# A graph layer whose last node tile is cut to the last two buckets, with x's product made in mid-run

## The chip, the cores and the metric

The kernel runs on one core of one Trainium2 chip. The metric is the device time of one launch in microseconds. The kernel before took 1346.37 us (median of 3 runs, 1346.32 to 1348.4).

## What is computed

6,250 nodes with 128 features, 206,250 edges with 128 features, float32 throughout. `src` is not sorted (the edges come sorted by `dst`), so the sum over edges is a scatter-add.

```python
def ref(x, edge_index, edge_features, global_feat, W_c, b_c, W1, b1, W2, b2, W3, b3):
    row = edge_index[0]                                   # src
    edge_aggr = jnp.zeros((n, HIDDEN)).at[row].add(edge_features)
    global_expand = jnp.repeat(global_feat, reps, axis=0)
    combined = jnp.concatenate([x, edge_aggr, global_expand], axis=-1) @ W_c + b_c
    h = jax.nn.softplus(combined @ W1 + b1)
    h = jax.nn.softplus(h @ W2 + b2)
    return h @ W3 + b3
x = _layernorm(x + ref(...), axis=-1)
```

## The kernel before

*Stages.* Nodes are split into 32 buckets of `BL` = 196. Stage one sorts the edges by bucket and puts them into DRAM (`rows_by`): edges are loaded in blocks (`load_rows`), a one-hot matrix per column of 122 edges is built on VectorE and ScalarE (`compare`, lines 973 to 982), TensorE multiplies by it (`gather`, 993), ScalarE copies the sorted columns out of PSUM (`settle`, 1005: four copies for a piece of up to three pairs of columns), and GpSimd scatters each pair of columns with one indirect DMA (`scatter_row`, 1022), 846 in all. Where each edge goes is worked out beside that in steps of VectorE and TensorE (`positions`). The 846 pairs are in eight groups of 28, 72, 124, 124, 124, 128, 124 and 122.

Stage two sums. Chunks of 128 sorted rows of one bucket are read back (`load`, on SyncE's queue), up to eight chunks a load. `match` (lines 811 to 826) compares each row's place in its bucket with the numbers 0 to 195 and so makes a 128 x 196 one-hot tile (`hot`), for units of up to four chunks; `product` (845) multiplies chunk by one-hot tile on TensorE into PSUM; `add` (866, 868) adds the result to `sums_t`, which is held features by nodes. A visit takes what is there of two neighbouring buckets. Stage two begins while stage one still runs; the last visits to each bucket come after the last scatter, in the order of buckets.

Stage three is the layer, in `node_layers` (1157). Since nothing nonlinear lies between `W_c` and `W1`, they are multiplied once (`combine`, into `fold`), and the biases likewise (`biases`). A tile is 512 nodes: 12 tiles of 512 and one of 106. A tile goes through `z_of(1)` (two products: `fold[:, 0]` with x turned, line 1168, `fold[:, 1]` with the sums, line 1169), `decay` and `log1p` on ScalarE (1179, 1180, 1185: exp and log of softplus), `softplus` on VectorE (1193, gives h), `z_of(2)` (1172), the same again, then `last_layer`: the third product (1208), x added (1212), mean and variance (1215, 1219). Tiles are normed in parts of three, three, three, two and two: `norm` works out 1/sqrt on VectorE in 12 tiny instructions (1228 to 1236) and then scales. All but the last part are scaled by GpSimd (1250) and stored from GpSimd's queue (1254); the last part is scaled by VectorE and ScalarE in turns (1250, 1247) and stored from SyncE's queue.

*Order.* TensorE, VectorE, ScalarE and SyncE run in the order in which the program emits. In stages one and two each step has a nominal time, worked out in the file, and the steps are emitted by it: a scatter every 1.3 us from 24 us on, `over(steps, t0, t1)` spreads a list evenly over a stretch. `PREP` = 0.85 keeps the last 15% of each group's stretch free of `positions`; with `NODES = (3, 4)` the steps of `node_rows`, `combine` and `biases`, go into the last 15% of group 3. `weights` loads the layer's weights and all of x turned (`x_t`) at a nominal 100 us. What is left of stage two after the last scatter (`rest`) is emitted tile by tile: `summed_to(k)` emits it until all buckets that tile k needs are summed.

One step of the layer loop emits: z2 of the tile before, `decay` and `log1p` of this tile and the one before, `summed_to` and z1 of the next tile, both `softplus`, and the last layer (and at a part's end the norm) of the tile two before. So norms of the first four parts stand between the sums of one tile and those of the next.

*SyncE's queue* carries all loads of edges and of chunks, the fill of `rows_by`, the weights and `x_t`; ScalarE's carries x for the residual (`x_sb`, read at the end of stage one as four runs of 512 bytes a partition).

The compare of one unit reads the numbers from PSUM:

```python
                    nc.vector.tensor_tensor(
                        hot[:, q - a:q - a + m],
                        chunks[j][:, lo:hi + 1:step, D:W].to_broadcast([P, m, BL]),
                        iota_ps.unsqueeze(1).to_broadcast([P, m, BL]), op=ALU.is_equal)
```

Of the kernel before, what the change touches and what calls it, by code (L numbers as in the profile page):

```python
# [7 lines left out]
F32 = mybir.dt.float32  # L8
# [10 lines left out]
P = 128  # L19

BL = 196
# [48 lines left out]
NODES = (3, 4)  # L70
TURNED = 2048
# [20 lines left out]
WEIGHTS = (("wc0", P), ("wc1", P), ("wc2", P), ("w1", P), ("w2", P), ("w3", P), ("b3", P), ("cols", 4))  # L92

# [39 lines left out]
def kernel(  # L133
# [11 lines left out]
    real_edges: int,  # L145
):
# [8 lines left out]
    N, D = x.shape  # L155
# [82 lines left out]
    x_t = const.tile([P, N], F32, name="x_t")  # L238
# [25 lines left out]

    def node_rows_of(pool, n0, n, bufs, load=sync_dma):
        t = pool.tile([P, 4, D], F32, name="x_sb", bufs=bufs)
        for lo, hi, r in blocks_of(n):
            m0 = n0 + lo * P
            load(t[:r, lo:hi, :],
                 x[m0:m0 + (hi - lo) * r, :].rearrange("(b p) d -> p b d", p=r))  # L270
        return t
# [11 lines left out]
    with ExitStack() as phase:  # L283
# [462 lines left out]
        def sum_steps():  # L746
# [64 lines left out]
            def match(n):  # L811
                j, a, e = units_of[n]
                hot = hots.tile([P, HALF, BL], F32, name="hot")
                hots_of[n] = hot
                q = a
                while q < e:
                    lo = hi = place_in(j, q)
                    step, m = 1, 1
                    while q + m < e and place_in(j, q + m) > hi and (m == 1 or place_in(j, q + m) == hi + step):
                        step, hi = place_in(j, q + m) - hi, place_in(j, q + m)  # L820
                        m += 1
# [4 lines that stand above are left out]
                    q += m  # L826
# [70 lines left out]
        def node_rows():  # L897
# [32 lines left out]
            return [combine, biases]  # L930
# [103 lines left out]
        with tc.manual_schedule(engines={ET.PE, ET.DVE, ET.Activation, ET.SP}):  # L1034
# [78 lines left out]
            when(100.0, weights)  # L1113
# [11 lines left out]
            for g in range(G):  # L1125
# [31 lines left out]
    def node_layers(sums, ready):  # L1157

        tiles = [(n0, min(4 * P, N - n0)) for n0 in range(0, N, 4 * P)]
        parts = [tiles[i:i + 3] for i in range(0, len(tiles) - 4, 3)]  # L1160
        parts += [tiles[len(parts) * 3:-2], tiles[-2:]]
# [3 lines left out]
        def z_of(layer, n0, w):  # L1165
            z = bank()
            if layer == 1:
                nc.tensor.matmul(z[:, :w], fold[:, 0, :], x_t[:, n0:n0 + w], start=True, stop=False)
                nc.tensor.matmul(z[:, :w], fold[:, 1, :], sums_t[:, n0:n0 + w],  # L1169
                                 start=False, stop=True)  # L1170
            else:
                nc.tensor.matmul(z[:, :w], w_sb["w2"], h1.pop(n0)[:, :w], start=True, stop=True)
            sub_z[layer, n0] = [z]

# [48 lines left out]
        def norm(now, last):  # L1223
# [13 lines left out]
            if last:  # L1237

                minus = work.tile([P, 16], F32, name="minus")[:, :nb]
                nc.vector.scalar_tensor_tensor(minus, mv[:, :nb, 0], -1.0, g,  # L1240
                                               op0=ALU.mult, op1=ALU.mult)
            for n0, w, y, at in now["done"]:
                for lo, hi, r in blocks_of(w):
                    for q in range(lo, hi):
                        k = at + q
                        if last and q % 2:
                            nc.scalar.activation(y[:r, q, :], y[:r, q, :], AF.Identity,
                                                 bias=minus[:r, k:k + 1], scale=g[:r, k:k + 1])
                            continue
                        (nc.vector if last else nc.gpsimd).tensor_scalar(  # L1250
                            y[:r, q, :], y[:r, q, :], mv[:r, k, 0:1], g[:r, k:k + 1],
                            op0=ALU.subtract, op1=ALU.mult)
                    m0 = n0 + lo * P
                    (sync_dma if last else nc.gpsimd.dma_start)(  # L1254
                        out[m0:m0 + (hi - lo) * r, :].rearrange("(b p) d -> p b d", p=r),
                        y[:r, lo:hi, :])


        with tc.manual_schedule(engines={ET.PE, ET.DVE, ET.Activation, ET.SP}):
# [14 lines left out]
            z_of(1, *tiles[0])  # L1274
            for step in range(len(tiles) + 2):
# [91 lines left out]
def laid_out(inputs):  # L1367
# [21 lines left out]
    return {"x": x, "x_turned": np.ascontiguousarray(x.T), "src": nodes, "src_runs": np.ascontiguousarray(  # L1389
# [23 lines left out]
```

## Time and profile before

| | |
|---|---|
| median of 3 runs | 1346.37 us |
| profiled execution | 1352.41 us |
| its span in the profile | 1350.7 us |
| busy: PE, PEld | 1199.8 us (89%), 1129.8 us (84%) |
| busy: DVE, ACT, POOL | 1020.2 us (76%), 1059.8 us (78%), 884.8 us (66%) |
| HBM read and written | 239.37 MB, 140.79 MB |

PE is TensorE's products and PEld its weight loads, DVE is VectorE, ACT ScalarE, POOL GpSimd, SP SyncE; a q behind a name is the queue of that engine, where DMAs are issued. A float32 product shows as two matmul records. A row of a timeline is: start in us from the span's start, length in us, engine, line, operation, output<-inputs, shapes, count; in brackets how long the engine was idle before it and which work ended that. A row may merge several instructions of one line. In a row of a group the first number after the bar is busy time in us, the second the mean length of one in ns. In a row of a stretch: from and to, its length, then busy us and count for each engine, the granted TensorE clock (1.00 is full), the DMA share and GB/s.

The span falls into two parts: until about 1108 us the scatters run on POOL; from there to the end the remaining sums and the layer run on PE, DVE and ACT.

### The profile page before, as it was taken

How to read it: one execution, taken by the hardware profiler on the slowest of the kernel's cores; microseconds unless marked ns; L12 is line 12 of the kernel's file. 1: busy time of each engine (PE TensorE's matmuls, PEld its weight loads, DVE VectorE, ACT ScalarE, POOL GpSimd, SP SyncE). 2: the span in 40 equal slices, each digit the busy share in tenths (PEclk: the TensorE clock that was granted, in tenths of full speed). 3: DMA queues.
4: the chain of work that ended last, by engine and by line, in shares of the span. 5: the costliest groups of instructions: out<-in, count | busy, mean ns of one | idle time of the engine just before them, and what ended most of it. 6: DMA issues, size and time to landing. Idle time of an engine off the chain costs nothing. (4 is left out here: it accounts for less than half of the span.)

```text
span 1350.7 us, 26938 instructions
## 1 busy us (share of the span) xinstructions
PE 1199.8 (89%) x8677; PEld 1129.8 (84%) x8677; DVE 1020.2 (76%) x2366; ACT 1059.8 (78%) x2469; POOL 884.8 (66%) x919
## 2 busy tenths in 40 slices
PE   5767788899988899998999999999999989998893
PEld 4666777889988889898998989989989988887782
DVE  7969757877788478896888877798656668777775
ACT  5999899999999879899899999989999930222222
POOL 2777777777777777777777777777777772003115
PEclk9889889999999889999999999999989999998996
DMA  9889999999989879998999989999999996545431
GB/s 242 259 265 368 344 351 341 340 336 339 311 293 307 279 257 304 294 321 286 304 317 293 339 288 292 308 297 323 332 337 312 330 297 207 171 149 152 126 118 51
DMA packets 196396, 377.48 MB, mean 279 GB/s; under 512 B 26038, under 2 KB 79870, under 8 KB 195866
## 3 DMA queue, kind: packets, MB, share of 16 engines
q1 hardware_dynamic: 148030, 255.64, 61.4%
q0 software_dynamic: 41488, 116.18, 24.6%
q10 hardware_dynamic: 6732, 3.87, 0.9%
q8 instruction: 73, 1.20, 0.4%
q14 instruction: 73, 0.60, 0.1%
HBM read 239.37 MB, written 140.79 MB: 281 GB/s over the span
## 5 line engine op out<-in xcount | busy, mean ns | idle before, releaser
L1022 POOL DMA_INDIRECT rows_by<-pairs,pair x846 | 826.0, 976 | 281.6 <-issue 201.3
L845 PE MATMUL part<-hot,chunks 128*128 128x196 f32 x3576 | 685.9, 338 | 20.3 <-DVE hot L822 13.4
L845 PEld LDWEIGHTS part<-hot,chunks 128*128 128x128 f32 x3576 | 600.2, 195 | 31.6 <-DVE hot L822 15.2
L1005 ACT COPY pairs<-sorted 64x387 f32<-64x387 f32 (+2 forms) x1144 | 543.5, 475 | 54.1 <-PE sorted L993 31.7
L993 PE MATMUL sorted<-rows,sort_hot 122*128 122x129 f32 x3384 | 504.2, 289 | 67.5 <-ACT pairs L1005 61.1
L993 PEld LDWEIGHTS sorted<-rows,sort_hot 122*128 122x128 f32 x3384 | 452.5, 199 | 89.7 <-ACT pairs L1005 86.1
L822 DVE TENSOR_TENSOR hot<-chunks,both_ps 128x392 f32<-128x392 f32 (+3 forms) x647 | 438.9, 710 | 30.5 <-PE part L845 19.4
L980 ACT ACTIVATE sort_hot<-plain,slot 122x128 f32<-122x128 f32 x846 | 278.3, 391 | 11.6 <-DVE slot L519 5.7
L868 DVE TENSOR_TENSOR sums_t<-sums_t,part 128x392 f32<-128x392 f32 (+1 forms) x163 | 89.5, 549 | 135.8 <-PE part L845 134.3
L982 ACT ACTIVATE sort_hot<-sort_hot,ones 122x384 f32<-122x384 f32 (+2 forms) x286 | 174.6, 610 | 9.3
L973 DVE TENSOR_TENSOR sort_hot<-slot,both_ps 122x384 f32<-122x384 f32 (+2 forms) x286 | 154.1, 541 | 13.5 <-PE sorted L993 7.5
L1179 ACT ACTIVATE away<-sorted,z_bias 128x512 f32<-128x512 f32 (+1 forms) x13 | 8.6, 660 | 184.2 <-PE sorted L1169 184.2
L1250 POOL TENSOR_SCALAR y<-y,mv,rs 128x128 f32<-128x128 f32 x44 | 34.3, 787 | 174.9 <-issue 102.4
L519 DVE TENSOR_REDUCE slot<-small 122x16 f32<-122x512 f32 (+2 forms) x109 | 72.9, 669 | 35.3 <-PE small L502 34.8
L623 DVE TENSOR_TENSOR past<-both_ps,starts 128x512 f16<-128x512 f32 (+2 forms) x110 | 71.9, 663 | 6.0 <-PE small L638 4.2
L441 DVE TENSOR_TENSOR pair_ib<-pair_block,both_ps 122x512 bf16<-122x512 bf16 (+2 forms) x109 | 71.7, 663 | 0.2
L502 PEld LDWEIGHTS <-starts_h 128*122 128x122 bf16 x423 | 43.0, 141 | 18.8 <-issue 9.9
L500 PE MATMUL small<-pair_ib,half 122*122 122x512 bf16 (+2 forms) x109 | 43.0, 394 | 7.2 <-DVE slot L519 7.2
L502 PE MATMUL small<-half,starts_h 128*122 128x128 bf16 x423 | 43.6, 226 | 0.0
L638 PEld LDWEIGHTS <-past 128*128 128x128 f16 x424 | 25.7, 99 | 18.9 <-DVE past L623 13.2
L638 PE MATMUL small<-jump,past 128*128 128x56 f16 (+3 forms) x424 | 29.2, 190 | 12.9 <-DVE past L623 9.6
L452 PE MATMUL small<-ones_h,pair_ib 122*128 122x48 bf16 x423 | 16.7, 186 | 12.7 <-DVE pair_ib L441 12.7
(128 smaller groups left out, 463.3 us busy)
## 6 DMA issues: line engine op xcount, KB each, us to landing
rows<-in_edge SPq DMA_DIRECT2D x105, 903.0 KB
chunks<-rows_by SPq DMA_DIRECT2D x158, 272.0 KB
chunks<-rows_by SPq DMA_DIRECT2D x60, 408.0 KB
chunks<-rows_by SPq DMA_DIRECT2D x69, 340.0 KB
chunks<-rows_by SPq DMA_DIRECT2D x131, 136.0 KB
rows_by<-pairs,pair POOLq DMA_INDIRECT x846
rows_by<-fill SPq DMA_DIRECT2D x21, 544.0 KB
rows<-in_edge SPq DMA_DIRECT2D x105, 80.6 KB
```

Of the source, the lines that this page charges most:

```text
L502: nc.tensor.matmul(pr[:, q * QUAD * NB:(q + 1) * QUAD * NB], own["starts_h"][:, q0 + q:q0 + q + 1].to_broadcast([KB, PN]), ident_h[:KB, :K ...
L519: nc.vector.tensor_reduce(to, of, axis=mybir.AxisListType.X, op=ALU.max)
L623: nc.vector.tensor_tensor(past[:, :, a:b], twice_ps[:KB].unsqueeze(1).unsqueeze(1).to_broadcast([KB, 2, b - a, P // 2]), own["starts"][:, ...
L822: nc.vector.tensor_tensor(hot[:, q - a:q - a + m], chunks[j][:, lo:hi + 1:step, D:W].to_broadcast([P, m, BL]), iota_ps.unsqueeze(1).to_bro ...
L845: nc.tensor.matmul(part[:, b - base_of[v], :], t[:, place_in(j, q), :D], hot[:, q - a], start=first, stop=last)
L868: nc.vector.tensor_add(here, here, of)
L973: nc.vector.tensor_tensor(hot[:PN, :m], slot[:PN, at:at + 2 * m - 1:2].unsqueeze(2).to_broadcast([PN, m, P]), slot_ps[:PN].unsqueeze(1).to ...
L980: nc.scalar.activation(hot[:PN, j], by_slot[:PN], AF.Abs, bias=slot[:PN, at:at + 1], scale=-1.0)
L982: nc.scalar.activation(hot[:PN, :m], hot[:PN, :m], AF.Relu, bias=ones[:PN, :1], scale=-1.0)
L993: nc.tensor.matmul(out[:, j, :], hot[:PN, j], rows_at[col // LOAD_COLS][:PN, col % LOAD_COLS, :], start=True, stop=True)
L1005: nc.scalar.copy(sets_at[i][64 * n:64 * n + 64, lo:lo + m, h, :W], out[64 * h:64 * h + 64, :m, :])
L1022: s = nc.gpsimd.indirect_dma_start(out=dst, out_offset=bass.IndirectOffsetOnAxis(ap=at, axis=0), in_=rows[:, j].rearrange("p a b -> p (a b ...
```

## The change

1. The node tiles: 11 of 512, one of 248 that ends where bucket 30 begins (node 5880), and a last one of 370 nodes, the last two buckets. Parts: four of three tiles, and the last tile alone.
2. x's product with `fold[:, 0]` leaves `z_of(1)`. It is made for 512 nodes at a time in mid-run (`times`), copied to SBUF as `x_f` (`times2`), and added to the product of the sums on VectorE (`with_x`) before ScalarE takes it; that addition is emitted behind the two `softplus` of the step before. x turned is loaded in 13 pieces (`fetch`), each two products ahead, into three buffers.
3. The steps of `node_rows` now go into the last 15% of groups 2 and 3: `combine`, two loads, `biases` and six products in group 2, seven products in group 3. The weights are loaded at a nominal 20 us.
4. Norms of the first four parts scale on ScalarE (an activation with scale and bias for each block of 128 nodes) and are stored from ScalarE's queue; GpSimd has no part in them. In the last part odd blocks are VectorE's and even ones ScalarE's.
5. Once all scatters are emitted, `match` makes one `tensor_scalar` for each chunk, with the numbers 0 to 195 in SBUF, where it made one `tensor_tensor` for up to four chunks.
6. x for the residual and the result lie in DRAM by blocks of 128 nodes, so that a tile's load or store is one run of up to 2 KB a partition. The host lays them out before and after.

```diff
-NODES = (3, 4)
-TURNED = 2048
+NODES, WEIGHTED = (2, 4), 20.0
+def node_tiles(n):
+    late = (-(-n // BL) - 2) * BL
+    assert 0 < n - late <= 4 * P
+    return [(a, min(4 * P, late - a)) for a in range(0, late, 4 * P)] + [(late, n - late)]
...
+    def in_blocks(of, n0, lo, hi, r):
+        at = next(k for k, (a, _) in enumerate(blocks) if a == n0 + lo * P) - lo
+        return of[:r, at + lo:at + hi, :]
...
+                if len(scattered) == TB:
+                    for q in range(a, e):
+                        at = place_in(j, q)
+                        nc.vector.tensor_scalar(hot[:, q - a], iota_f[:, :BL], chunks[j][:, at, D:W],
+                                                None, op0=ALU.is_equal)
+                    return
...
-            return [combine, biases]
+            of = {}
+            spans = [(a, min(N, a + 4 * P)) for a in range(0, N, 4 * P)]
+
+            def fetch(k):
+                a, b = spans[k]
+                of[k] = per.tile([P, 4 * P], F32, name="x_turned", bufs=3)[:, :b - a]
+                sync_dma(of[k], x_turned[:, a:b])
+
+            def times(k):
+                small = small_bank().rearrange("p b n -> p (b n)")[:, :spans[k][1] - spans[k][0]]
+                nc.tensor.matmul(small, fold[:, 0, :], of.pop(k), start=True, stop=True)
+                of["times", k] = small
+                if k + 2 < len(spans):
+                    fetch(k + 2)
+
+            def times2(k):
+                nc.vector.tensor_copy(x_f[:, slice(*spans[k])], of.pop(("times", k)))
+
+            steps = [combine, lambda: fetch(0), lambda: fetch(1), biases]
+            for k in range(len(spans)):
+                steps += [lambda k=k: times(k), lambda k=k: times2(k)]
+            return steps
...
-                for a in range(0, N, TURNED):
-                    b = min(N, a + TURNED)
-                    sync_dma(x_t[:, a:b], x_turned[:, a:b])
...
-            when(100.0, weights)
+            when(WEIGHTED, weights)
...
-                    upto = len(nodes)
+                    upto = len(nodes) if g + 1 == NODES[1] else 4 + (len(nodes) - 4) // 4 * 2
...
-        tiles = [(n0, min(4 * P, N - n0)) for n0 in range(0, N, 4 * P)]
-        parts = [tiles[i:i + 3] for i in range(0, len(tiles) - 4, 3)]
-        parts += [tiles[len(parts) * 3:-2], tiles[-2:]]
+        tiles = node_tiles(N)
+        parts = [tiles[i:i + 3] for i in range(0, len(tiles) - 1, 3)] + [tiles[-1:]]
...
-                nc.tensor.matmul(z[:, :w], fold[:, 0, :], x_t[:, n0:n0 + w], start=True, stop=False)
-                nc.tensor.matmul(z[:, :w], fold[:, 1, :], sums_t[:, n0:n0 + w],
-                                 start=False, stop=True)
+                nc.tensor.matmul(z[:, :w], fold[:, 1, :], sums_t[:, n0:n0 + w], start=True, stop=True)
...
+        def with_x(n0, w):
+            z = work.tile([P, 4 * P], F32, name="z_x", bufs=3)
+            nc.vector.tensor_add(z[:, :w], sub_z[1, n0][0][:, :w], x_f[:, n0:n0 + w])
+            sub_z[1, n0] = [z]
...
                         if last and q % 2:
+                            nc.vector.tensor_scalar(y[:r, q, :], y[:r, q, :], mv[:r, k, 0:1],
+                                                    g[:r, k:k + 1], op0=ALU.subtract, op1=ALU.mult)
+                        else:
                             nc.scalar.activation(y[:r, q, :], y[:r, q, :], AF.Identity,
                                                  bias=minus[:r, k:k + 1], scale=g[:r, k:k + 1])
-                            continue
-                        (nc.vector if last else nc.gpsimd).tensor_scalar(
-                            y[:r, q, :], y[:r, q, :], mv[:r, k, 0:1], g[:r, k:k + 1],
-                            op0=ALU.subtract, op1=ALU.mult)
-                    m0 = n0 + lo * P
-                    (sync_dma if last else nc.gpsimd.dma_start)(
-                        out[m0:m0 + (hi - lo) * r, :].rearrange("(b p) d -> p b d", p=r),
-                        y[:r, lo:hi, :])
+                    (sync_dma if last else nc.scalar.dma_start)(
+                        in_blocks(out, n0, lo, hi, r), y[:r, lo:hi, :])
...
                 for layer, tile_ in ((1, first), (2, second)):
                     if tile_:
                         softplus(layer, *tile_)
+                if step + 1 < len(tiles):
+                    with_x(*tiles[step + 1])
```

More of the change, by code (lines that the diff above doesn't have):

```diff
@@ L145 @@
     real_edges: int,
+    n_nodes: int,
 ):
     nc = tc.nc
-    N, D = x.shape
+    N, D = n_nodes, x.shape[2]
+    blocks = node_blocks(N)
     E = src.shape[0]
@@ L236 @@
     cols = of_weights["cols"]
-    x_t = const.tile([P, N], F32, name="x_t")
+    x_f = const.tile([P, N], F32, name="x_f")
     fold = const.tile([P, 2, D], F32, name="fold")
@@ L1236, in norm @@
                 nc.vector.scalar_tensor_tensor(g, t, 1.5, g, op0=ALU.add, op1=ALU.mult)
[L1237 to L1241, printed above, removed]
+            minus = work.tile([P, 16], F32, name="minus", bufs=2)[:, :nb]
+            nc.vector.scalar_tensor_tensor(minus, mv[:, :nb, 0], -1.0, g, op0=ALU.mult, op1=ALU.mult)
             for n0, w, y, at in now["done"]:
@@ L1274, in node_layers @@
             z_of(1, *tiles[0])
+            with_x(*tiles[0])
             for step in range(len(tiles) + 2):
```

21 lines of the change are left out of this document (14 added, 7 removed).

## The prediction

> **What bounds the kernel now.** First the groups and the waits, to see who sets the pace while edges are still being sorted. Columns of a group: busy us, mean ns | idle before, releaser.
>
> ```profile
> span 1350.7 us, 26938 instructions
> L1022 POOL DMA_INDIRECT rows_by<-pairs,pair x846 | 826.0, 976 | 281.6 <-issue 201.3
> POOL rows_by L1022 <- DVE much L585: 23.0, 2, 22.7
> ```
>
> The 846 scatters take (826.0 + 281.6 - 23.0) / 846 = 1.282 us each, and beyond the 23.0 us at the start POOL waits for almost nothing: its gaps are its own issue. So POOL sets the pace until the last scatter at 1107.9. Next the stretches (length, then busy us of PE, PEld, DVE, ACT, POOL; granted clock, DMA share, GB/s):
>
> ```profile
> 1000.00:1050.00 50.00, 49.58 (x347) 48.39 (x345) 33.34 (x57) 48.26 (x114) 38.10 (x40) 1.00 0.98 323
> 1140.00:1320.00 180.00, 168.19 (x883) 149.51 (x882) 133.85 (x286) 41.75 (x64) 23.44 (x30) 0.96 0.48 146
> ```
>
> After the scatters PE is busy 93% and DVE 74%: PE sets the tail. The timeline shows one step of it (start, length, engine, line, idle before):
>
> ```profile
> 1305.68 0.56 DVE L868 TENSOR_TENSOR sums_t<-sums_t,part 128x392 f32<-128x392 f32 x1 [1.07 <-PE part L845]
> 1306.47 1.02 PE L1168 MATMUL sorted<-x_t,fold 128*128 128x512 f32 x2
> 1307.33 1.02 PE L1169 MATMUL sorted<-sums_t,fold 128*128 128x512 f32 x2
> 1308.19 1.05 PE L1208 MATMUL small<-weights_sb,h 128*128 128x128 f32 x8
> 1309.08 1.02 PE L1172 MATMUL sorted<-h,weights_sb 128*128 128x512 f32 x2
> 1309.28 0.69 DVE L1212 TENSOR_TENSOR y<-small,x_sb 128x512 f32<-128x512 f32 x1 [1.72 <-PE small L1208]
> 1309.94 1.16 PE L845 MATMUL part<-hot,chunks 128*128 128x196 f32 x6
> 1311.07 1.41 DVE L822 TENSOR_TENSOR hot<-chunks,both_ps 128x588 f32<-128x588 f32 x2
> 1311.91 6.21 PE L845 MATMUL part<-hot,chunks 128*128 128x196 f32 x36 [0.81 <-PE part L845]
> ```
>
> A 512-wide product holds PE 0.86 us (1306.47 to 1307.33), a chunk 2 x 6.21 / 36 = 0.345 us. At a step's end DVE adds, forms both h, waits 1.72 us for the last-layer product, and only then makes the hot tiles that PE needs. Once the sums are done (the add at 1318.15) a latency chain runs to the end:
>
> ```profile
> 1318.15 0.56 DVE L868 TENSOR_TENSOR sums_t<-sums_t,part 128x392 f32<-128x392 f32 x1 [2.42 <-PE part L845]
> 1341.56 0.88 ACT L1247 ACTIVATE y<-y,minus,rs 128x128 f32<-128x128 f32 x2 [10.38 <-DVE minus L1240]
> 1342.46 0.88 SPq L259 DMA_DIRECT2D out<-y  x2
> 1344.79 0.81 POOL L1254 DMA_DIRECT2D out<-y  x1 [0.30 <-POOL y L1250]
> ```
>
> POOL is last, 2.3 us after SP; from its end (1345.6) to the end of the span are 5.1 us.
>
> **The change, part by part.** *x's product leaves the tail.* PE drops one 0.86 us product per tile; for the ten tiles 0 to 9 that is -8.6 us. DVE gains one addition per tile (`with_x`), by the row of L1212 0.69 us. It fits: the product taken away shortens DVE's 1.72 us wait to 0.86, and the addition needs only the first product, done before the second h. So DVE, too, reaches `y` 0.86 us earlier, and the whole step moves forward. What hides the addition is that wait; without it each step would give 0.69 back. Bounds: -8.6 with the cover whole, -1.7 with none; I take -8.6, since the wait stands in every step with a last layer.
>
> *The product's new place.* 13 products (11 us of PE), 13 copies out of PSUM (by L1212 some 0.69 us each) and 13 loads on SP's queue come into the last 15% of groups 2 and 3, six in the first window (about 291 to 315 us) and seven in the second; combine and biases move there from the second. POOL is the bound there, so the cost is nothing while sorted pairs are ahead of it. Counting ACT's copies (four for a piece of three pairs; 136 copies hold the first 100 pairs) against scatters started, from the windows of those two lines:
>
> ```profile
> 0.00:300.00 300.00, 142.05 (x298) 0.93 0.98 316
> 0.00:300.00 300.00, 209.61 (x215) 0.93 0.98 316
> 290.00:300.00 10.00, 9.12 (x60) 8.43 (x60) 5.03 (x10) 9.68 (x25) 7.56 (x9) 1.00 1.05 356
> 300.00:310.00 10.00, 8.48 (x61) 8.48 (x62) 6.07 (x13) 9.63 (x24) 7.56 (x9) 1.00 1.06 342
> 460.00:470.00 10.00, 8.71 (x59) 8.38 (x57) 1.93 (x8) 8.54 (x21) 7.56 (x9) 0.93 0.84 275
> 467.13 0.16 DVE L917 TENSOR_TENSOR z_bias<-small,weights_sb 128x1 f32<-128x1 f32 x1 [9.17 <-PE small L916]
> 469.03 0.29 DVE L928 TENSOR_TENSOR b_all<-small,weights_sb 128x128 f32<-128x128 f32 x1 [0.58 <-PE small L927]
> ```
>
> 100 + 3 x 162 / 4 = 221.5 pairs are copied at 300 us, 215 scatters started: six pairs, 7.7 us ahead. Six products (5.2 us) and the bias chain (some 2 us, from 467.1 to 469.0) less PE's 2.4 us of slack in 20 us put PE about 5 us behind. A wait on an SP load would come on top: PE stands at `times(k)` with the sorting behind it, which ACT's copies and then POOL need. Loads are asked for two steps, about 6 us, ahead. Bounds 0 to +7; I take 0, since the lead is larger than what is counted. The weights' load moves from 98.8 us to about 13 us, needed only at 291: nothing. In place of one load of x at 99 us the same bytes come in 13: nothing, POOL did not wait then or now.
>
> *One compare per chunk in the tail.* `match` replaces one instruction for up to four chunks, with the table in PSUM, by one `tensor_scalar` per chunk with the table in SBUF. Nearest is another one-pointer `tensor_scalar` on f32 in SBUF, among `tensor_tensor` of the same size:
>
> ```profile
> 15.81 0.24 DVE L609 TENSOR_SCALAR jump<-plain,far 128x56 f16<-128x56 f32 x1
> 15.97 0.21 DVE L605 TENSOR_TENSOR jump<-earlier,plain 128x56 f16<-128x56 f32 x1
> 567.76 0.34 DVE L609 TENSOR_SCALAR jump<-plain,far 128x256 f16<-128x256 f32 x1
> 568.02 0.42 DVE L605 TENSOR_TENSOR jump<-earlier,plain 128x256 f16<-128x256 f32 x1
> 568.36 0.35 DVE L609 TENSOR_SCALAR jump<-plain,far 128x256 f16<-128x256 f32 x1
> 1300.40 4.21 DVE L822 TENSOR_TENSOR hot<-chunks,both_ps 128x588 f32<-128x588 f32 x7
> ```
>
> From its start to the next one's: 0.16 us for 56 columns, 0.26 for 256, so 0.13 + 0.0005 a column; 196 columns take 0.23 us. `tensor_tensor` takes 0.34 for 256 (568.02 to 568.36), twice the slope. Today seven instructions make 18 chunks in 4.21 us, 0.234 each. A tie: 0. [...]
>
> *Norms and stores on ACT.* For each of the four whole parts ACT gets 10 or 12 scale-and-bias activations and the stores; POOL gets none. Two L1247 in 0.88 us, the second about 0.39 after the first: 12 x 0.39 + three stores at 0.44 issue (SP's two took 0.88) and a short drain, 0.55 each: 6.4 us. Norms 1 and 2 come ahead of the next steps' six activations in ACT's order; those need 4.1 us and are due after 42 chunks (14.5 us), so 10.5 us is covered. The third is not covered: it sits before the last activations.
>
> *The end, laid out anew.* The 12th tile (248 nodes) needs only buckets to 29, the 13th the last two. PE's order becomes: six chunks, product of the 12th, last layer of the 9th, z2 of the 11th, 15 chunks of the last two buckets, product of the 13th. Twelve of those 15 wait for hot tiles that DVE makes behind the third norm, and the last sums, the 13th's product and all of the end wait for them. A norm today:
>
> ```profile
> 1276.81 0.17 DVE L1235 SCALAR_TENSOR_TENSOR rs<-rs 128x12 f32<-128x12 f32 x1
> 1277.01 0.17 DVE L1236 SCALAR_TENSOR_TENSOR rs<-rs 128x12 f32<-128x12 f32 x1
> 1277.92 16.17 PE L845 MATMUL part<-hot,chunks 128*128 128x196 f32 x78 [3.33 <-DVE hot L822]
> 1318.63 0.75 DVE L1193 SCALAR_TENSOR_TENSOR h<-sorted,neg_z,away 128x512 f32<-128x512 f32 x1
> 1319.94 0.69 ACT L1179 ACTIVATE away<-sorted,z_bias 128x512 f32<-128x512 f32 x1 [7.45 <-PE sorted L1169]
> 1321.95 0.67 ACT L1179 ACTIVATE away<-sorted,b_c 128x512 f32<-128x512 f32 x1
> ```
>
> PE stands 3.33 us and then makes 78 matmuls in 16.17 us where 36 take 6.21: 2.7 us lost to the clock too. In today's clock, from the add at 1305.68 on: h of the 10th and 11th tiles, its z addition, `y` and statistics bring DVE to 1316.6, the norm (13 at 0.205) to 1319.3; first hot unit 1320.1; PE, idle 3.9 us and then slow, ends the 12 chunks about 1327.2 (1318.1 today). ACT norms from 1319.3 to 1325.9, then two activation triples (1.4 us for 248 columns, 2.05 for 512, as 1319.94 to 1321.95) to 1329.35, which is later than PE: h to 1330.05, z of the 13th 1330.6, its triple (1.7) 1332.3, the 12th's 1333.75, `y` of the 11th 1336.15, h of the 13th 1336.75, two blocks 1338.5, norm 1341.2, three blocks 1343.2, norm 1346.0; ACT meanwhile norms ten blocks with four stores (6 us) to 1347.2, two more blocks 1348.1, SP's stores to about 1348.7. That is 3.1 us after POOL's 1345.6. With the same 5.1 us behind it: +3.1. Bounds: +0.8 (today's end need not have waited for SP, whose last store left 2.3 us before POOL's, so 5.1 us behind it may be 2.8) to +6 (0.44 for each activation and 0.88 for each store, in both last norms).
>
> Sum: -8.6 + 0 + 0 + 3.1 = -5.5 us on the 1350.7 us span, 1345.2. The profiled execution took 1352.4 in all, 6.0 over the median of 1346.37; the runs should move by the same -5.5: 1340.9.
>
> **Rivals.** [...]
>
> ```profile
> [...]
> 24.12 0.28 DVE L569 TENSOR_SCALAR most_of<-much 128x1 f32<-128x1 f32 x3
> 48.97 0.15 DVE L569 TENSOR_SCALAR most_of<-much 128x1 f32<-128x1 f32 x1
> ```
>
> [...]
>
> B, no change: mid-run stall. If the loads of x land later than 6 us, each makes PE stand; 1.5 us at each of 13 uses up the lead by some 9 + 5 - 7.7 = 6.3 us in a window, and POOL never catches up: 1347. For: DMA share 1.05 there. Against: the lead.
>
> C, faster: a compare costs only 0.065 beside its columns, as a one-column L569 does (three in 0.28, one in 0.15), so 0.065 + 0.10 = 0.17. Hot units come 0.19 us sooner in ten steps: -1.9, 1339.0. [...]
>
> D, it does not do what it says: PE's freed time is given back to DVE's in-order waits; only the end's +3.1 stays: 1349.5.
>
> **Chances.** Forecast 0.52 (its own range 1336 to 1345), A 0.10, B 0.14, C 0.14, D 0.10. Range 1335 to 1351: it leaves out A and the edges of the forecast. A difference under 0.2% (2.7 us) can't be told from none. Faster 0.70 (forecast, C and some of B), same 0.12 (most of B), slower 0.18 (A, D).
>
> **What will show it.** The last scatter still ends at 1108 +-1 (else B). A tail step loses 0.86 us of PE with no new wait. [...] ACT's third norm ends after PE's last chunk, the last chunk ends near 1318.6, about where it ends now, and the last store leaves SP near 1340. I am wrong if the step before the third norm does not come some 8 us earlier, or if the stretch from the last chunk to the end does not shrink from 32.6 us to about 27.

## The result and the profile after

| | before | after |
|---|---|---|
| median of five runs, us | 1348.4 (1346.32 to 1348.99) | 1360.59 (1355.11 to 1362.0) |
| after / before, 95% interval | | 1.0077 (1.0056 to 1.0099) |
| span of the profiled execution, us | 1350.7 | 1360.0 |
| last scatter ends, us | 1108.9 | 1121.4 |
| from there to the end of the span, us | 241.8 | 238.6 |
| from the start of the last addition to the sums to the end, us | 32.6 | 24.7 |

The change made the kernel 0.77% slower; 1340.9 us was forecast, with a range of 1335 to 1351. Against the profile of before, the scatters end 12.5 us later, and what follows them is only 3.2 us shorter. First the group of the scatters in the kernel after (busy us, mean ns | idle before):

```profile
L1062 POOL DMA_INDIRECT rows_by<-pairs,pair x846 | 825.4, 976 | 294.8 <-issue 204.5
```

The scatters' waits for ACT's copies before (us in all, times, the longest):

```profile
POOL rows_by L1022 <- ACT pairs L1005: 15.0, 48, 0.7
```

And in the kernel after, with a wait of PE:

```profile
POOL rows_by L1062 <- ACT pairs L1045: 30.0, 57, 1.6
...
PE part L864 <- DVE hot L832: 23.7, 5, 14.0
```

POOL's own work is as before (825.4 us); its idle time grew from 281.6 to 294.8 us, and its waits for ACT's copies of sorted pairs from 15.0 to 30.0. The last line is another place: 14.0 us in one wait of PE for a hot tile. The timeline of the kernel after shows both (start, length, engine, line, idle before):

```profile
293.00 1.45 SPq L270 DMA_DIRECT2D x_turned<-in_x_turned  x1
...
302.42 2.08 PE L959 MATMUL small<-x_turned,fold 128*128 128x512 f32 x2 [5.46 <-DMA x_turned<-in_x_turned]
...
305.82 0.97 ACT L1045 COPY pairs<-sorted 64x387 f32<-64x387 f32 x2 [6.32 <-PE sorted L1033]
...
1120.23 16.96 DVE L832 TENSOR_SCALAR hot<-plain,chunks 128x196 f32<-128x196 f32 x6
1120.36 1.03 POOL L1062 DMA_INDIRECT rows_by<-pairs,pair  x1 [0.30 <-issue]
1121.47 15.37 POOL L1303 TENSOR_TENSOR x_sb<-x_sb,b_all 128x512 f32<-128x512 f32 x15
1136.59 5.66 PE L864 MATMUL part<-hot,chunks 128*128 128x196 f32 x24 [14.03 <-DVE hot L832]
...
1317.80 0.69 DVE L1251 TENSOR_TENSOR y<-small,x_sb 128x512 f32<-128x512 f32 x1 [0.27 <-PE small L1247]
...
1335.29 0.56 DVE L887 TENSOR_TENSOR sums_t<-sums_t,part 128x392 f32<-128x392 f32 x1 [4.71 <-PE part L864]
```

In mid-run, the first piece of x is asked for at 293.00 and its product can start only at 302.42: PE stands 5.46 us, with the sorting queued behind it, makes the product in 2.08 us where a fast one takes 1.02, and ACT's copies stand 6.32 us. At the head of the tail six compares take 16.96 us where six take 1.45 to 1.47 later on; one of them alone is 15.6 us long. Meanwhile GpSimd makes 15 additions in a row, 1121.47 to 1136.84: b3 is added to each tile's x for the residual (before has the same additions, 13 of them). All instructions of these two lines (duration in ns: least, median, longest; first and last start in us):

```profile
L832 DVE TENSOR_SCALAR hot<-plain,chunks x460: 286/314/15605, 1112.2 to 1330.3; 128x196 f32<-128x196 f32 x154
L1303 POOL TENSOR_TENSOR x_sb<-x_sb,b_all x15: 442/1250/1293, 1121.5 to 1136.4; 128x512 f32<-128x512 f32 x11, 128x128 f32<-128x128 f32 x1, 120x128 f32<-120x128 f32 x1, 128x256 f32<-128x256 f32 x1
```

The long compare is over when the last addition has just begun (1136.4), and PE, which needs its hot tile, goes on at 1136.59 after standing 14.03 us. The last addition to the sums shows the end: 24.7 us from its start to the end of the span.

### The profile page after: what moved, and what is told of

It reads as the page before. It is cut to its first block, busy times and chain, and to the rows that moved or that the text cites. A ratio compares the mean times of both kernels' runs of the same rounds, so it can differ in the third digit from the quotient of the medians.

```text
span 1360.0 us, 27273 instructions
## 1 busy us (share of the span) xinstructions
PE 1201.4 (88%) x8677; PEld 1132.5 (83%) x8677; DVE 1053.5 (77%) x2685; ACT 1079.4 (79%) x2515; POOL 841.4 (62%) x866
## 4 chain that ended last, share of the span: by engine, by line
PE 38%; DVE 8%; ACT 6%; DMA 6%; issue 3%; POOL 2%; ACTq 0%; SPq 0%; DVEq 0%; POOLq 0%
PE part L864 26%; PE sorted L1033 10%; ACT pairs L1045 3%; DMA chunks<-rows_by 3%; DMA rows_by<-pairs,pair 2%; POOL rows_by L1062 2%; DVE hot L832 2%; ACT sort_hot L1020 1%; DVE hot L841 1%; PE sorted L1204 1%; DMA rows<-in_edge 1%; ACT y L1286 1%; PE small L1247 1%; DVE stats L1254 0%; PE small L515 0%
## 5 line engine op out<-in xcount | busy, mean ns | idle before, releaser
L1062 POOL DMA_INDIRECT rows_by<-pairs,pair x846 | 825.4, 976 | 294.8 <-issue 204.5
L841 DVE TENSOR_TENSOR hot<-chunks,both_ps 128x392 f32<-128x392 f32 (+3 forms) x475 | 329.5, 717 | 26.6 <-PE part L864 17.4
L832 DVE TENSOR_SCALAR hot<-plain,chunks 128x196 f32<-128x196 f32 x460 | 126.6, 348 | 0.2 <-DMA chunks<-rows_by 0.2
L1218 ACT ACTIVATE away<-z_x,z_bias 128x512 f32<-128x512 f32 (+2 forms) x13 | 9.1, 696 | 136.7 <-DVE z_x L1211 135.4
L1286 ACT ACTIVATE y<-y,minus,rs 128x128 f32<-128x128 f32 (+2 forms) x48 | 20.0, 483 | 41.2 <-DVE minus L1277 37.0
```

Of the source, the lines that this page charges most:

```text
L832: nc.vector.tensor_scalar(hot[:, q - a], iota_f[:, :BL], chunks[j][:, at, D:W], None, op0=ALU.is_equal)
L841: nc.vector.tensor_tensor(hot[:, q - a:q - a + m], chunks[j][:, lo:hi + 1:step, D:W].to_broadcast([P, m, BL]), iota_ps.unsqueeze(1).to_bro ...
L1062: s = nc.gpsimd.indirect_dma_start(out=dst, out_offset=bass.IndirectOffsetOnAxis(ap=at, axis=0), in_=rows[:, j].rearrange("p a b -> p (a b ...
```

## Experiments

Each ratio is against runs of before on the same chip at the same time, with its 95% interval. "Last scatter" is its end in the one profile that each kernel has. e5, c1 to c3, g1 and g2 ran on chips on which every kernel, before too, took some 1680 us; in their profiles POOL waited 312 to 337 us for ACT's copies (15 in the profile of before); why, no run shows. From them only the head of the tail is read.

| kernel | what it is | median us | ratio to before | last scatter, us |
|---|---|---|---|---|
| after | the change | 1360.59 | 1.0077 (1.0056 to 1.0099) | 1121.4 |
| e1 | after, old compare | 1351.39 | 1.0000 (0.9979 to 1.0022) | 1116.9 |
| e2 | after, x's product in the layer | 1360.47 | 1.0078 (1.0049 to 1.0106) | 1109.1 |
| e3 | e2, old compare: end and norms alone | 1349.68 | 0.9993 (0.9977 to 1.0009) | 1109.8 |
| e4 | after, x loaded in bulk | 1351.03 | 1.0001 (0.9983 to 1.0020) | 1114.1 |
| f3 | e4, old compare | 1341.91 | 0.9946 (0.9928 to 0.9964) | 1111.5 |
| f1 | f3, the products spread out | 1337.33 | 0.9913 (0.9892 to 0.9935) | 1108.4 |
| f2 | as f1, spread earlier | 1338.66 | 0.9925 (0.9897 to 0.9953) | 1109.7 |
| f4 | f3 without the products | 1340.25 | 0.9927 (0.9898 to 0.9956) | 1109.8 |
| h1 | f1, new compare from the first layer on | 1335.84 | 0.9886 (0.9867 to 0.9905) | 1110.9 |
| h2 | after, new compare from the first layer on | 1344.72 | 0.9965 (0.9944 to 0.9986) | 1118.9 |
| c1 | e2 without GpSimd's additions | 1677.12 | 0.9968 (0.9935 to 1.0001) | |
| c2 | e2, table in PSUM | 1689.10 | 1.0049 (1.0020 to 1.0079) | |
| c3 | e2, two inputs in SBUF | 1686.35 | 1.0026 (0.9998 to 1.0055) | |
| e5 | as f1 | 1673.50 | 0.9960 (0.9931 to 0.9990) | |
| g1 | as h1 | 1661.53 | 0.9922 (0.9894 to 0.9950) | |
| g2 | as h2 | 1667.41 | 0.9956 (0.9929 to 0.9983) | |

### The two causes apart: e1 to e4

e1 takes the new compare out, e2 takes x's product back into the layer, e3 does both, e4 only loads x in bulk, and the weights with it, as before does:

```diff
-                if len(scattered) == TB:            # e1, e3: these lines go
-                    for q in range(a, e):
...
-            def fetch(k):                           # e4: no pieces
...
-                nc.tensor.matmul(small, fold[:, 0, :], of.pop(k), start=True, stop=True)
+                nc.tensor.matmul(small, fold[:, 0, :], x_f[:, a:b], start=True, stop=True)
...
                 sync_dma(weights_sb, weights_in)
+                for a in range(0, N, 2048):
+                    sync_dma(x_f[:, a:min(N, a + 2048)], x_turned[:, a:min(N, a + 2048)])
...
-            when(WEIGHTED, weights)
+            when(100.0, weights)
```

> The changed kernel with the compare of before everywhere (one two-input compare for up to four chunks, table in PSUM), all else kept. Theory: the single compare that stood for 15.6 us stood because VectorE's one-input SBUF compare cannot run beside GpSimd's 13 additions of x and b3; with the other form no instruction of VectorE lasts over 2 us, the last scatter stays at 1121 +-1, and some 10 to 14 us go: 1348 +-3. Rival: the compare waited for something else (a late load of sorted rows, the end of the scatters); then the two-input compare waits as long and the time stays at 1360.

> The changed kernel with x's product put back into the layer (x loaded in bulk at about 99 us, accumulated in PSUM, no addition on VectorE), the one-input compare and the new end kept. Theory: the loss in mid-run comes from x's product and its loads; last scatter back at 1109 +-1, the 15 us compare stays, the tail gets 8.6 us of products back: 1360.6 - 12.5 + 8.6 = 1357. Rival: the scatters are late for another part of the change (x's rows laid out by tiles, their loads, the earlier load of the weights): last scatter stays at 1121, 1369.

> The end laid out anew, the norms on ScalarE and the layouts alone: x's product in the layer and the two-input compare as before. Theory: no stall at either place, last scatter 1109 +-1, and the stretch from the last sums' addition to the end is 25 us where it was 32.6: 1348.4 - 7.6 = 1341. Rival, the prediction's own sum: the end costs 3.1 us: 1351.

> The changed kernel with x turned loaded in bulk at about 99 us into the buffer that the product later overwrites; the 13 products and 13 copies stay in the same two windows, the one-input compare stays. Theory: PE stood for the loads of the pieces, and not for the work; last scatter at 1110 +-2, 1360.6 - 11 = 1350. Rival: the 13 products, copies and the small PSUM buffers themselves cost the lead; last scatter stays at 1118 or later, 1357 to 1360.

The timeline of e1 at the place of the stall:

```profile
1117.00 15.44 POOL L1297 TENSOR_TENSOR x_sb<-x_sb,b_all 128x512 f32<-128x512 f32 x15
...
1121.90 17.00 PE L858 MATMUL part<-hot,chunks 128*128 128x196 f32 x86 [2.46 <-issue]
...
1123.03 1.44 DVE L835 TENSOR_TENSOR hot<-chunks,both_ps 128x588 f32<-128x588 f32 x2
```

That of e2:

```profile
1108.86 16.80 DVE L833 TENSOR_SCALAR hot<-plain,chunks 128x196 f32<-128x196 f32 x6
1109.24 15.37 POOL L1283 TENSOR_TENSOR x_sb<-x_sb,b_all 128x512 f32<-128x512 f32 x15
...
1219.13 4.23 DVE L833 TENSOR_SCALAR hot<-plain,chunks 128x196 f32<-128x196 f32 x18
1219.48 7.23 PE L865 MATMUL part<-hot,chunks 128*128 128x196 f32 x42 [0.39 <-DVE hot L833]
```

That of e3:

```profile
1205.24 1.02 PE L1185 MATMUL sorted<-h,weights_sb 128*128 128x512 f32 x2
...
1207.30 4.18 DVE L836 TENSOR_TENSOR hot<-chunks,both_ps 128x588 f32<-128x588 f32 x7
...
1208.09 7.23 PE L859 MATMUL part<-hot,chunks 128*128 128x196 f32 x42 [0.83 <-DVE hot L836]
...
1217.77 1.02 PE L1185 MATMUL sorted<-h,weights_sb 128*128 128x512 f32 x2
...
1301.05 0.56 DVE L882 TENSOR_TENSOR sums_t<-sums_t,part 128x392 f32<-128x392 f32 x1 [1.07 <-PE part L859]
...
1315.70 5.93 PE L859 MATMUL part<-hot,chunks 128*128 128x196 f32 x24 [3.54 <-DVE hot L836]
...
1341.80 0.78 SPq L271 DMA_DIRECT2D out<-y  x2
```

And of e4:

```profile
1114.24 15.39 POOL L1299 TENSOR_TENSOR x_sb<-x_sb,b_all 128x512 f32<-128x512 f32 x15
1114.31 16.36 DVE L832 TENSOR_SCALAR hot<-plain,chunks 128x196 f32<-128x196 f32 x6 [0.34 <-DMA chunks<-rows_by]
```

With the two-input compare, which reads its table from PSUM, VectorE works beside the additions and PE waits 2.46 us. With the one-input compare the stall comes in every kernel, wherever the additions fall: from 1108.9 in e2, 1114.3 in e4, 1120.2 in after. The rival of e1, a late load, is out. e1 gained 0.77%, 10 us, the lower end of what was expected. The rows also size the stall: the layer's first product starts 53.4 us after the last scatter in after and e2 and 54.1 in e4, but 39.1 to 42.7 us after it in e1, e3, f1 to f4, h1 and h2.

e2's last scatter is back at 1109.1, so the mid-run loss comes from x's product. Its time was to be 3.6 us under that of after and is the same (1.0078 against 1.0077), which their intervals allow. e4's 1114.1 shows that the pieces' loads are only part of it: in its first window PE waits for no load of x, and still 5 us are lost. The expectation for e4's scatter (1110 +-2) missed; the loads and the work both count.

e3, expected at 1341, took 1349.68: the change's end by itself is worth nothing that can be told (-0.07%, -0.23 to +0.09). The expectation was read off the stretch after the last addition to the sums (24.7 us), but the third norm, now ahead of the last chunks, delays that addition: PE stands 3.54 us behind it at 1315.70.

### What locks the compare out: c1 to c3

All three are e2 with one edit. c1 leaves out GpSimd's additions, and so the bias b3; c2 and c3 change the compare:

```diff
-                        nc.vector.tensor_scalar(hot[:, q - a], iota_f[:, :BL], chunks[j][:, at, D:W],
-                                                None, op0=ALU.is_equal)
+                        nc.vector.tensor_scalar(hot[:, q - a], iota_ps, chunks[j][:, at, D:W],        # c2
+                                                None, op0=ALU.is_equal)
+                        nc.vector.tensor_tensor(hot[:, q - a], iota_f[:, :BL],                        # c3
+                                                chunks[j][:, at, D:W].to_broadcast([P, BL]), op=ALU.is_equal)
```

> e2 (one-input compare, x in the layer) without GpSimd's additions of x and b3: b3 is left out of the result. Theory: the 15 us compare waits for GpSimd's run of additions, so it goes with them; no compare over 1 us, PE idles under 5 us between 1105 and 1130, and the time is that of e3, 1350. Rival: the compare waits for a load of sorted rows or for the scatters' end; it stays at about 15 us and the time at 1360.

> e2 with the one-input compare reading its table from PSUM, GpSimd's additions kept. [...] Rival: any one-input compare with its pointer in SBUF is locked out; the 15 us stay.

> e2 with one two-input compare per chunk, both inputs in SBUF, GpSimd's additions kept. [...] Rival: any instruction of VectorE with all its inputs in SBUF is locked out; one of them stands for 15 us.

The timeline of c1 in the first 20 us after the scatters, where GpSimd has nothing to do:

```profile
1433.35 1.46 DVE L833 TENSOR_SCALAR hot<-plain,chunks 128x196 f32<-128x196 f32 x6
```

That of c2:

```profile
1433.81 11.80 POOL L1283 TENSOR_TENSOR x_sb<-x_sb,b_all 128x512 f32<-128x512 f32 x12 [0.80 <-DMA x_sb<-in_x]
1433.89 2.06 DVE L833 TENSOR_SCALAR hot<-both_ps,chunks 128x196 f32<-128x196 f32 x6
```

That of c3:

```profile
1430.11 15.51 POOL L1283 TENSOR_TENSOR x_sb<-x_sb,b_all 128x512 f32<-128x512 f32 x15
1430.16 1.64 DVE L842 TENSOR_TENSOR hot<-chunks,both_ps 128x588 f32<-128x588 f32 x2
...
1432.18 0.14 DVE L1141 CAST many_i<-many_f 1x1 int32<-1x1 f32 x1
...
1433.39 12.72 DVE L833 TENSOR_TENSOR hot<-plain,chunks 128x196 f32<-128x196 f32 x3
...
1445.37 6.87 PE L865 MATMUL part<-hot,chunks 128*128 128x196 f32 x24 [9.95 <-DVE hot L833]
```

Without the additions there is no stall (c1: no compare over 0.33 us). With the table in PSUM there is none either (c2), though a compare then takes 0.34 us (six in 2.06). In c3 a two-input compare with both inputs in SBUF stands as well, for 11.9 us until 1445.3, when the last addition is under way, while the one with its table in PSUM runs beside them at 1430.16. So it is not the one-input form; of the three compares, those that read only SBUF are locked out, and this is what "lockout" means below. By c1 the additions are needed for it. In after and e2 the stuck compare was due to end 0.23 and 0.07 us before the first addition starts by the trace; what held it in that moment stays open.

Not every VectorE instruction that reads SBUF alone is locked out. In c3 the conversion of one number from SBUF to SBUF (1432.18) takes 0.14 us in the middle of the additions. And near the end of before, where GpSimd scales y, VectorE's norm runs beside it on tiles of 5 and 8 columns, some of it with two inputs in SBUF:

```profile
1333.90 2.37 POOL L1250 TENSOR_SCALAR y<-y,mv,rs 128x128 f32<-128x128 f32 x3
...
1334.05 0.17 DVE L1234 TENSOR_TENSOR rs<-rs 128x8 f32<-128x8 f32 x1
...
1334.45 0.32 DVE L1236 SCALAR_TENSOR_TENSOR rs<-rs 128x8 f32<-128x8 f32 x1
```

These take 0.17 us, as they do with GpSimd idle (1276.81 in before), now and then up to 0.33. Whether the size matters, or that GpSimd's instruction has one tensor as input here and two in the additions, no run shows.

Nor does any run show what it is that holds the compare back. It waits for more than one instruction: in after VectorE stood through a run of back-to-back additions up to its last one, 15.6 us where one addition takes 1.25 at the median.

### What the products cost in mid-run: f1 to f4

f1 and f2 keep e4's bulk load and take the old compare; they spread the products evenly (f1 over 200 to 500 us, f2 over 130 to 300), f3 has the two bursts of the change (six and seven products), f4 leaves out the products and their copies, so that x itself is added in place of its product:

```diff
+            nodes, of_x = node_rows()
+            over(nodes, 190.0, 200.0)
+            for k, (one, two) in enumerate(of_x):
+                at = 200.0 + (k + 0.5) / len(of_x) * 300.0
+                when(at, one)
+                when(at + 2.0, two)
```

> x loaded in bulk at about 99 us, its 13 products one every 23 us from 200 to 500 us instead of in two bursts, the two-input compare; the rest as in the changed kernel. Theory: a burst of seven bank-wide products and the bias chain used up the pairs ahead and PE has too little slack to win them back, while one product per 23 us fits into the slack; last scatter at 1110 +-1.5, and with the 231 us that e1 needed from the last scatter to the end the span is 1341 and the time 1343, 0.6% under before. Rival: PE has no slack for the products wherever they stand; last scatter at 1114 as in e4, time 1347.

> The kernel of e5 once more, since its chip made every kernel, before too, some 330 us longer than all other runs. Theory, where before takes about 1350: one product per 23 us fits into PE's slack; last scatter at 1110 +-1.5, 231 us from it to the end, 0.6% under before. Rival: PE has no slack for the products wherever they stand: last scatter at 1114, 0.3% under before.

> As f1, the products one every 13 us from 130 to 300 us, where PE is busy 80 to 88%. Theory: if any slack will do, the same as f1, last scatter at 1110 +-1.5. Rival: only five pairs are ahead there, and the products take them; last scatter at 1113 or later.

> As f1 with the two bursts of e4 (x in bulk, two-input compare). Theory: last scatter at 1114 +-2 and 231 us to the end, 1346, 0.3% under before; slower than f1 by some 4 us. Rival: the bursts of e4 cost nothing and its 1114 was chance; the same as f1.

> As f3 without the 13 products and their 13 copies (x itself is added in place of its product). Theory: what is left, the bias chain at 291 us and the bulk load, costs no pairs; last scatter at 1110 +-1, over ten pairs ahead at 400 us as in before. Rival: the early bias chain or the waits between its steps eats the lead; last scatter at 1113 or later and under seven pairs ahead at 400 us.

The first 400 us, instructions of ACT's copy line and of POOL's scatter line (length, busy us, their count, granted clock, DMA share, GB/s). Before, a stretch that the prediction didn't read:

```profile
0.00:400.00 400.00, 193.95 (x408) 0.94 0.98 315
...
0.00:400.00 400.00, 285.81 (x293) 0.94 0.98 315
```

After:

```profile
0.00:400.00 400.00, 187.15 (x394) 0.91 0.97 307
...
0.00:400.00 400.00, 281.44 (x288) 0.91 0.97 307
```

f3, the bursts:

```profile
0.00:400.00 400.00, 189.79 (x400) 0.92 0.97 313
...
0.00:400.00 400.00, 285.16 (x293) 0.92 0.97 313
```

f1, spread:

```profile
0.00:400.00 400.00, 191.69 (x404) 0.93 0.97 315
...
0.00:400.00 400.00, 285.36 (x293) 0.93 0.97 315
```

f4, none:

```profile
0.00:400.00 400.00, 193.28 (x407) 0.95 0.98 315
...
0.00:400.00 400.00, 284.84 (x292) 0.95 0.98 315
```

By the prediction's count (100 pairs in the first 136 copies, three pairs in four copies after that) the pairs ahead at 400 us are 100 + 0.75 x 272 - 293 = 11.0 in before, 11.3 in f4, 8.0 in f1, 5.0 in f3, and 5.5 in after, which by then has scattered five fewer. The waits of POOL for copies between 500 and 760 us (us in all, times, the longest), in f3:

```profile
POOL rows_by L1050 <- ACT pairs L1033: 6.8, 14, 1.1
```

And in f1:

```profile
POOL rows_by L1047 <- ACT pairs L1030: 2.4, 8, 0.3
```

The longest counts here, and not the sum: a scatter's usual gap is 0.3 us, and f4, which has no products, has 6.1 us in waits of at most 0.3. By the starts of the scatters, f3 falls 2.7 us further behind before between its 481st and its 521st (641 to 692 us), and the other four kernels with bursts (after, e1, e4, h2) 2.7 to 2.9, the kernels without at most 0.1. So the bursts don't stop POOL in their own window; they take its lead, the pairs sorted ahead, and later hitches that the lead would have hidden become waits. f1's last scatter (1108.4) is as early as f4's: spread out, 13 products and copies cost nothing. f2 is as good, so its rival (only five pairs ahead there) fell. f3's 1111.5 lies half a microsecond under the range expected for it.

f1 also came out faster than expected (0.9913, not 0.994): from last scatter to the end 225.7 us, where e1 had needed 230.9. f2 to f4 need 226.6 to 227.0, so it was e1's profile that was long there.

### The compare outside the lockout: g1, g2, h1, h2

```diff
-                if len(scattered) == TB:
+                if summed["to"] >= 4 * P:
```

g1 and h1 are f1 with this, g2 and h2 the changed kernel with nothing but this:

> f1 with the one-input compare of the change, but only from the first layer on (its first tile's sums complete, some 25 us after GpSimd's additions are over); until then the two-input one. Theory: outside the additions the one-input compare is a gain, since PE's step from one z2 product to the next was 0.44 us shorter with it in e2 than in e3 (12.10 against 12.54): seven to ten such steps, so 3 to 4.5 us below f1, 0.9887 of before, and no compare over 1 us. Rival: at the same 0.236 us a chunk it gains nothing in the end: the same as f1, 0.991.

> The changed kernel whole, x's pieces and bursts as they are, with only the start of the one-input compare moved as in g1. Theory: the lockout costs the changed kernel 8 to 12 us, all of it beside GpSimd's additions, so this stands 0.8% under the changed kernel, at 0.997 to 1.000 of before (1.000 in e1, less the 3 us by which the compare gains later). Rival: the lockout is hidden by rows of the sums that are late anyway (PE waited 4 us there in e3): over 1.004.

> The kernel of g1 once more, whose chip made every kernel, before too, some 330 us longer. Theory, where before takes about 1350: 0.9885 of before (f1's 0.9913 less 3 to 4.5 us), PE's steps from z2 to z2 11.25 us where f1's are 11.69. Rival: the same as f1, 0.991.

> The kernel of g2 once more, for the same reason. Theory: no VectorE instruction stands beside GpSimd's additions; the mid-run loss stays (last scatter 1115 to 1122); 0.997 to 1.000 of before. Rival: over 1.004.

The timeline of h1, with two z2 products, a step apart:

```profile
1203.34 1.02 PE L1196 MATMUL sorted<-h,weights_sb 128*128 128x512 f32 x2
...
1214.57 1.02 PE L1196 MATMUL sorted<-h,weights_sb 128*128 128x512 f32 x2
```

The same step of f1:

```profile
1200.51 1.02 PE L1190 MATMUL sorted<-h,weights_sb 128*128 128x512 f32 x2
...
1212.18 1.02 PE L1190 MATMUL sorted<-h,weights_sb 128*128 128x512 f32 x2
```

h2 answers what the lockout cost: 1.0077 - 0.9965 = 1.1% of 1350, 15 us (+-4, from the two intervals), and without it the change is faster than before. h1 is the fastest kernel of all, 1.14% under before. Its 0.27% over f1 lies inside their intervals (+-0.29), so the medians alone don't settle the gain; the rows do. A step from z2 to z2 takes 1214.57 - 1203.34 = 11.23 us in h1 and 1212.18 - 1200.51 = 11.67 in f1, and e2 and e3 show where that is from: 18 hot tiles take the same time (4.23 and 4.18 us), but PE waits 0.39 us for the first of them with one compare per chunk, and 0.83 with one for three.

## Why the prediction was wrong, point by point

**"What bounds the kernel now"** held: POOL's pace until the last scatter, PE in the tail.

**"x's product leaves the tail", -8.6 us: right.** f1's step from z2 to z2 is 11.67 us where e3's is 1217.77 - 1205.24 = 12.53: 0.86 us a step. VectorE's wait for the last layer fell as worked out, to 0.27 us in after (1317.80), with the addition inside it. f1 against e3, which differ by x's product and the place of the bias chain, gives 0.80% +-0.27: 10.8 us +-3.6, and 8.6 lies in it.

**"The product's new place", "I take 0, since the lead is larger than what is counted": failed.** Three parts of that step were wrong. A load asked for "about 6 us ahead" was there only after 9.4 us at 293.00, and PE stood 5.46; "in place of one load of x at 99 us the same bytes come in 13: nothing" was thus wrong. The lead of six pairs was read at the start of the first window and taken as given; in before it grew from there to 11 pairs at 400 us, and the later hitches need it, so using it up "for nothing" had a price even where no load is late (f3 against f1: 0.33% +-0.28). And what was lost was never won back. Loading in pieces cost 0.54% more (e1 against f3, +-0.28, the weights' earlier load included). Together (e1 against f1) 0.87%, some 12 us. The scatters' 12.5 us in the profile of after is the worst of three: e1 and h2, the same up to the last scatter, lose 8.1 and 10.1. They differ in the wait for the first piece of x, 1.37 us in e1, 3.06 in h2 and 5.46 in after. Rival B had this mechanism with its place, at half the size (6.3 us): its 1.5 us a load was guessed, and the shrinking lead afterwards wasn't in it.

**"One compare per chunk", "a tie: 0": failed, by what was left out.** The duration was right: 4.23 / 18 = 0.235 us a chunk where 0.23 was worked out from two rows, against 0.234. A, the slower rival, stood for twice L609's slope, 0.13 + 196 x 0.001 = 0.33 us a chunk; a price like that appears only with the table in PSUM (c2: 0.34). But the price was taken from VectorE alone. The edit also moved an input from PSUM to SBUF, in the one stretch of the changed kernel in which GpSimd computes, and that cost 15 us. The profile of before had the row that warns of it, GpSimd's 13 additions right behind the last scatter, where the new compare comes in:

```profile
1108.95 15.13 POOL L1270 TENSOR_TENSOR x_sb<-x_sb,b_all 128x512 f32<-128x512 f32 x13
```

No rival had it. The small gain, 0.44 us in a step and in seven steps some 3 us, is rival C's effect, hot tiles sooner, with another cause.

**"The end, laid out anew", +3.1 us: too high.** From the addition before the norm (1301.05 in e3, 1305.68 in before) the norm was forecast to let PE go on 14.4 us later, and it did after 14.65; the last store was to leave SP 43.0 us later and left after 41.5; behind it come 3.9 us where 5.1 were taken. The activation triple read as 2.05 us takes 2.01 by the rows named for it. No run shows the short drain that the forecast added to each store's 0.44 us on ACT: in after the issue takes 0.34 to 0.37 us, and ACT's scaling stands 0.42 to 0.45 us for a store where 0.55 was taken. The 78 matmuls of before that gave the slow pace of PE ran at a granted clock of 0.81 (1277.92 to 1294.09), the 36 at 1.00 (1311.91 to 1318.12); in e1, after 3.54 us of waiting each time, 78 take 16.06 us once and 13.20 us once. In all 45.45 us in e3 against 45.0 before, +0.4, under the bound of +0.8. e3's interval (-3.1 to +1.2 us) shuts +3.1 out.

**What would show it.** "The last scatter still ends at 1108 +-1 (else B)": 1121.4, so B. The step lost its 0.86 us. Three compares took 0.69 us from start to start, three times the 0.23 that was forecast. ACT's third norm was to end after PE's last chunk, which contradicts the prediction's own working (norm to 1325.9, chunks to 1327.2); the runs agree with the working: 1333.6 against 1335.2 in after, 1320.8 against 1321.6 in e3. The product of the step before that norm was to come some 8 us earlier; the same product (the 11th tile's) starts at 1315.8 in after, 9.3 us later than before (1306.47), as the scatters' delay and the lockout came first. The stretch from the last addition to the end shrank to 24.7 us, not 27.

Without the lockout the change's time is h2's, 0.35% under before; the prediction's -5.5 us are 0.41%. That they agree is partly luck: in h2 10 us of mid-run loss (the last scatter at 1118.9) are offset by an end 2.7 us and a compare some 3 us better than forecast, and by two places where the one profile of before is long. The layer's first product starts 45.3 us after the last scatter there and 39.9 in h2: in between, VectorE waited 4.8 us for loads of sorted rows (2.9 in h2), and 86 matmuls in a row took 18.11 us (15.61 in h2). And the two steps that hold the first two norms (23.81 and 23.96 us from z2 to z2, 21.58 and 19.90 in h2) are longer by 3.7 us than the products and the compare explain. What of this belongs to the change and what to a single profile stays open.

## What to carry to other kernels

Price an edit not only by its instruction's own duration but by where its operands lie and what every other engine does in the same microseconds: a compare that reads SBUF alone, at the same price by itself, stood 15 us beside GpSimd's additions. A lead that pays for later hitches is not free slack; work put into mid-run should be spread over the whole time in which the pacing engine has pairs ahead, and loaded long before. After a change with several parts, take the parts back one by one: what f1 keeps was worth 0.87%, and the compare and the way in which x was loaded and multiplied had buried it.

## What the runs showed of the hardware

A VectorE compare of 196 columns that reads only SBUF waited through a run of GpSimd's `tensor_tensor` instructions until the last had begun (15.6 us, after; 12 us, c3), and not only for the one in progress; one with an input in PSUM ran beside the same run at its usual speed (0.34 us a compare in c2, 1.64 us for two in c3 as in c1). The conversion of one number within SBUF did not wait (0.14 us, c3), nor did instructions on 5 to 8 columns beside GpSimd's `tensor_scalar` (0.17 to 0.33 us, before). For one compare of 196 columns the kinds differ: 0.245 us one-input from SBUF, 0.285 two-input from SBUF, 0.34 one-input with the table in PSUM (each from six in a row). And one kernel took 1337 us on one chip and 1673 on another (f1 and e5), with POOL's scatters at 0.975 us each on both.
